# A Mamba scan whose input comes from TensorE in 32-row quarters, four states into four banks

## The chip, the cores and the metric

The kernel runs on one core of a Trainium2 chip. The metric is device time in microseconds (us) of one execution, all phases included. Three runs of the kernel before took 3399.39, 3389.66 and 3397.66 us (median 3397.66).

## The reference, cut to what matters

Two transformer-like layers work on x, 8 sequences of 512 tokens of 256 features. Layer 0 adds to x a Mamba block and an FP4-quantized feed-forward of the normalized x; layer 1 adds a block-sparse attention and a two-deep local attention with its own feed-forward. The change touches the Mamba block (512 inner channels, 16 states, rank 16) and what shares its phase:

```python
u = silu(conv(x_in))                              # [b, l, 512]
x_dbl = u @ W_xproj.T                             # rank 16 | B 16 | C 16
delta = softplus(x_dbl[..., :16] @ W_dt.T + b_dt)
A = -exp(A_log)
def step(h, inp):                                 # one token
    dA = exp(d_t[:, :, None] * A[None])
    h = dA * h + (d_t * u_t)[:, :, None] * B_t[:, None, :]
    y_t = einsum('bdn,bn->bd', h, C_t)
    return h, y_t
y = (ys + D_param * u) * silu(z)
out = y @ W_out.T
```

So for each sequence, channel and state a first-order recurrence runs over 512 tokens. Its input is delta times u (which depends on channel and token) times B (which depends on state and token).

## The kernel before, in words

**Two phases.** Phase one (lines 114 to 796) computes layer 0 for all eight sequences and writes x1 to DRAM. Phase two (from line 799) computes layer 1. They share no work. The diff touches phase one alone.

**The scan.** Channels lie on the 128 partitions, so a sequence has 4 chunks of 128 channels (NC). One step `g` handles two states of one chunk: 8 steps a chunk, STEPS = 32 a sequence, 256 in all. For a step, `decay` (line 655) makes two tiles `da` = exp(delta * A) on ScalarE (ACT); `spread_b` (663) spreads one row of B over all partitions into a PSUM bank, by one bf16 matmul of 512 columns with a selecting matrix `sel`, where B lies in `bp` as three bf16 pieces that add up to its float32 value; `product` (669) multiplies each bank in place by `du` = delta * u on VectorE (DVE); `scan` (677) runs the recurrence on DVE from `da` and the bank into `hh`; `times_c` (680) multiplies both states by C on GpSimd (POOL), where C comes by a broadcast DMA into `cb`; `sum_states` (683) adds the states up by 8 transposes (128x128) on TensorE (PE) into the bank `y`, which turns them to rows.

**The strands.** Everything else of phase one is written as Python generators: `head` (layer norm, input projection, convolution, `xd`, delta and `du` by two chunks at a time), `ffn` (the FP4 feed-forward), `z`, `finish`, `output`, `fp4_weights`, `rotary_tables`. The main loop (765 to 796) calls `step()` once for each scan step; `step` asks every active strand for its next stage, if PSUM banks are free for it (MM = 4 banks in `pmm`; `bu` has 3, `y` one). The wrapper `Ordered` keeps each engine's instructions in the order in which this loop issues them. So every engine's queue is fixed, and an instruction that waits holds up all behind it on its engine. In a loop pass the order around the scan is: `fetch_c(g+2)`, `sum_states` of an older step, `decay(g+1)`, first scan, `spread_b(g+1)` twice, `step()`, `times_c(g-1)`, second scan, `product(g+1)`.

Delta, `du` and u of a sequence are each one tile of 4 chunks, double-buffered. x is loaded once and held until `output` is done with it.

Of the kernel before, what the change touches and what calls it, by code (L numbers as in the profile page):

```python
# [17 lines left out]
P = 128  # L18
NB, L, D = 8, 512, 256
NT = L // P  # L20
# [16 lines left out]
RD, RC, PIECES = 32, 48, (0, 64, 96)  # L37
# [18 lines left out]
def tile_kernel(ctx: ExitStack, tc: tile.TileContext, a: dict, out: bass.AP):  # L56
# [57 lines left out]
    with ExitStack() as s0:  # L114
# [6 lines left out]
        MM = 4  # L121
        pmm = s0.enter_context(tc.tile_pool(name="pmm0", bufs=MM, space=PSUM))
        pbu = s0.enter_context(tc.tile_pool(name="pbu0", bufs=3, space=PSUM))
# [5 lines left out]
        def load_x(b):  # L129
            t = w1.tile([P, NT, D], FP, tag="x", bufs=3, name=f"x_{b}")  # L130
            sp.dma_start(t, a["x"][b].rearrange("(t p) d -> p t d", p=P))
            return t

        x_first = load_x(0)
# [5 lines left out]
        w_dt = w0.tile([RD + DR, DI], FP, name="w_dt")  # L140
        sp.dma_start(w_dt[RD:, :], a["w_dt"])
# [3 lines left out]
        w_o = load(w0, chunks(a["w_o"]), [P, NC, D], "w_o")  # L145


        sel = w0.tile([P, NS, P], BF, name="sel")
        every = w0.tile([P, NS], BF, name="every")

        def constants():
            act.activation(a_neg, a_neg, AF.Exp)
            dve.tensor_scalar(a_neg, a_neg, -1.0, None, ALU.mult)
            dve.tensor_copy(every, ident[:, :NS])
            for at in PIECES[1:]:
                dve.tensor_tensor(every, every, ident[:, at : at + NS], ALU.add)
            for n in range(NS):
                dve.tensor_copy(sel[:, n, :], every[:, n : n + 1].to_broadcast([P, P]))

# [3 lines left out]
        w_d = w0.tile([P, NI, D], FP, name="w_d")  # L163

# [159 lines left out]
        def rotary_tables():  # L328

            for l in range(DEPTH):  # L330
                tab = rot.tile([P, 2, L], FP, tag="e", bufs=2, name="tab")
                tab = tab.rearrange("p i (t d) -> p (i t) d", d=LD).rearrange("p (i t) d -> p i t d", t=NT)
                sp.dma_start(tab, a["rotary"])
                qss = []
                for name in ("q_scale", "k_scale"):
                    qss.append(sm.tile([P, LD], FP, tag="qs", bufs=2, name="qs"))
                    sp.dma_start(qss[-1], a[name][l].unsqueeze(0).to_broadcast([P, LD]))
                yield 0, 0
                yield 0, 0
                dve.tensor_scalar(qss[0], qss[0], 8.0, None, ALU.mult)  # L340
                hd = LD // 2
                lo, hi = slice(0, hd), slice(hd, LD)
                for i, qs in ((0, qss[0]), (2, qss[1])):
                    for at, cols, sc in ((i, lo, lo), (i, hi, hi), (i + 1, lo, hi), (i + 1, hi, lo)):
                        by = qs[:, sc].unsqueeze(1).to_broadcast([P, NT, hd])
                        dve.tensor_tensor(tab[:, at, :, cols], tab[:, at, :, cols], by, ALU.mult)
                        if cols is hi:
                            yield 0, 0
                sp.dma_start(tab_d[l], tab)
                yield 0, 0  # L350

        made, xs, u_, z_, ready, through = {}, {}, {}, {}, set(), set()

        def head(b):

            x = xs[b] = load_x(b) if b else x_first
# [12 lines left out]
            dve.reciprocal(rs, rs)  # L369
            xn = w1.tile([P, NT, D], FP, tag="xn", name="xn")  # L370
# [56 lines left out]
            def silu(c, cv):  # L427
                if c == 0:
                    u_[b] = w1.tile([P, NC, L], FP, tag="u", name="u")
                act.activation(u_[b][:, c, :], cv, AF.Silu)  # L430

            stages = [(project, 0, 1), tap0, taps12, (tap3, 1, 0), silu]
            for i, need in enumerate(skewed(range(NC), stages, 2)):
                while i + 1 == len(stages) and b - 2 in u_:
                    yield 0, 0
                yield need
            u = u_[b]
            yield 1, 1
            ps = pmm.tile([P, L], FP, tag="mm", name="ps_xp")
            for c in range(NC):  # L440
                pe.matmul(ps, w_xp[:, c, :], u[:, c, :], start=(c == 0), stop=(c == NC - 1))
            yield 0, -1
            xd = w1.tile([P, L], FP, tag="xd", bufs=1, name="xd")
            act.copy(xd, ps)
            c_d = dram.tile([NS, L], FP, tag="c_d", name="c_d")
            sp.dma_start(c_d, xd[RC : RC + NS, :])

            bp = w1.tile([P, L], BF, tag="bp", name="bp")
            act.copy(bp, ps)
            yield 0, 0  # L450

            def pieces():
                for at in PIECES[1:]:
                    pool.tensor_tensor(xd[at:, :], xd[at:, :], bp[at:, :], ALU.subtract)
                    yield 0, 0
                    act.copy(bp[at:, :], xd[at:, :])
                    yield 0, 0

            delta = w1.tile([P, NC, L], FP, tag="delta", name="delta")
            du = w1.tile([P, NC, L], FP, tag="du", name="du")
            made[b] = xn, xt, bp, c_d, delta, du

            def rank(c):
                ps = pmm.tile([P, L], FP, tag="mm", name="ps_dt")
                pe.matmul(ps, w_dt[RD:, c * P : (c + 1) * P], xd[RD : RD + DR, :], start=True, stop=True)
                return ps

            def parts(c, ps):  # L470
                act.activation(delta[:, c, :], ps, AF.Relu, bias=b_dt[:, c : c + 1])
                act.activation(ps, ps, AF.Abs, bias=b_dt[:, c : c + 1])
                act.activation(ps, ps, AF.Exp, scale=-1.0)
                act.activation(du[:, c, :], ps, AF.Copy, bias=1.0)
                return ps

            def rests(c, e, ps):
                w = du[:, c, :]
                dve.scalar_tensor_tensor(e[:, c % 2, :], w, 1.0, ps, ALU.subtract, ALU.subtract)

            def second(c0, ps):
                return ps, rank(c0 + 1)

            def third(c0, st):
                e = rot.tile([P, 2, L], FP, tag="e", bufs=2, name="e")
                rests(c0, e, st[0])
                return e, parts(c0 + 1, st[1])

            def fifth(c0, st):
                rests(c0 + 1, *st)  # L490
                return st[0]

            def logs(c0, e):
                w = du[:, c0 : c0 + 2, :]
                act.activation(w, w, AF.Ln)
                return e

            def sums(i):
                def f(c0, e):
                    w = du[:, c0 + i, :]  # L500
                    by.tensor_tensor(w, w, e[:, i, :], ALU.subtract)
                    return e
                return f

            def deltas(i):
                def f(c0, e):
                    c = c0 + i
                    by.tensor_tensor(delta[:, c, :], delta[:, c, :], du[:, c, :], ALU.add)
                    by.tensor_tensor(du[:, c, :], delta[:, c, :], u[:, c, :], ALU.mult)
                    ready.add((b, c))  # L510
                    return e
                return f

            by = pool if b else dve
            rest = pieces()
            stages = [
                (lambda c0, _: rank(c0), 0, 1), parts, (second, 0, 1), (third, 1, 0), lambda _, st: st, (fifth, 1, 0),
                logs, sums(0), sums(1), deltas(0), deltas(1),
            ]
            for need in skewed(range(0, NC, 2), stages, 2 if b else len(stages) - 4):  # L520
                next(rest, None)
                yield need

        def ffn(b):

            x, xn = xs[b], made[b][0]
# [21 lines left out]
            yield from skewed(range(KC), [(turn_x, 0, 1), (put_x, 1, 0)], 1)  # L548
            n = FI // 2
# [30 lines left out]
            def down(t, ht):  # L580
                ps = pmm.tile([P, L], FP, tag="mm", name="ps_d")
                for c in range(NI):
                    m = min(P, FI - c * P)
                    pe.matmul(
                        ps[:, :D], ht[:m, c, :], w_d[:m, c, :], start=(c == 0), stop=(c == NI - 1)
                    )
                return ps

            def add(t, ps):
                dve.tensor_tensor(x[:, t, :], x[:, t, :], ps[:, :D], ALU.add)  # L590

            def begin(t, _):
# [6 lines left out]
                *to_inner(lambda t: q.tile([P, NI, P], FP, tag="ht", name="ht")), (down, 0, 1), (add, 1, 0),  # L599
            ]  # L600
            yield from skewed(range(NT), stages, 5)
# [10 lines left out]
        def output(b):  # L612

            u, x = u_[b], xs[b]

            def tile(i):
                def f(t, ps):
                    if i == 0:
                        ps = pmm.tile([P, L], FP, tag="mm", name="ps_o")
                    for c in range(NC):  # L620
                        pe.matmul(
                            ps[:, i * D : (i + 1) * D], u[:, c, (t + i) * P : (t + i + 1) * P], w_o[:, c, :],
# [7 lines left out]
            def add(t, ps):  # L630
                at = x[:, t : t + 2, :].rearrange("p t d -> p (t d)")
# [4 lines left out]
            yield from skewed(range(0, NT, 2), [(tile(0), 0, 1), tile(1), (add, 1, 0)], 2)  # L636
# [13 lines left out]
        def fetch_c(g):  # L650
            b, c, n = at(g)
            cs[g] = rot.tile([P, 2, L], FP, tag="cb", bufs=3, name="cb")
            sp.dma_start(cs[g], made[b][3][n : n + 2, :].unsqueeze(0).to_broadcast([P, 2, L]))

        def decay(g):
            b, c, n = at(g)
            decays[g] = []
            for i in range(2):
                da = rot.tile([P, L], FP, tag="da", bufs=4, name="da")
                act.activation(da, made[b][4][:, c, :], AF.Exp, scale=a_neg[:, c, n + i : n + i + 1])  # L660
                decays[g].append(da)

        def spread_b(g, i):
            b, c, n = at(g)
            bu = pbu.tile([P, L], FP, tag="bu", name="bu")
# [811 lines left out]
```

## Time and profile before

| | |
|---|---|
| runs, us | 3399.39, 3389.66, 3397.66 |
| profiled execution, span from first to last instruction | 3396.9 us |
| that span beside the median of the runs | 0.8 us below it |
| end of phase one (last add into x, write of x1) | about 1398 us |
| first scan starts, last scan starts | 45.4 us, 1374.5 us |
| mean granted TensorE clock | 0.942 (0.87 up to 1400 us, 0.99 from there) |
| busy to 1400 us: PE, DVE, ACT, POOL | 1042.9, 1256.4, 962.8, 1036.2 us |
| busy from 1400 us: PE, DVE, ACT, POOL | 1931.1, 1166.0, 808.6, 545.3 us |
| 242 ACT table loads in phase one | 1.283 us each |

The page gives the busy time of each engine, the span in 40 slices with a digit for tenths, the chain of work that ended last, and groups of equal instructions. In a group, "busy" is the time that the group's instructions cover, with overlaps counted once; "mean" is one instruction from its start to its end. For pipelined matmuls busy divided by count is far below mean, and it is the better price of one more of them. A float32 matmul appears in the trace as two matmuls, each with its weight load; a transpose as one.

### The profile page before, as it was taken

To read this page: it belongs to the slowest core of one execution; us is meant where nothing else is said; L and a number is where in the kernel's file an instruction comes from. 1 tells how busy PE (TensorE), PEld (TensorE's weight loads), DVE (VectorE), ACT (ScalarE), POOL (GpSimd) and SP (SyncE) were. 2 spreads that over 40 slices of the span, in tenths; PEclk is the share of its full clock that TensorE was granted. 3 is DMA by queue.
4 is the path that set the end of the run, shared out by engine and by line. 5 is a ranking of instruction groups with operands and counts; after the bars stand their busy time and mean duration, and the time that the engine had idled before them with its cause. 6 is when DMAs were issued, how large, how long until landed. Compare 5 with 4: busy or idle time off the path is not lost.

```text
span 3396.9 us, 43346 instructions
## 1 busy us (share of the span) xinstructions
PE 2974.0 (88%) x15235; PEld 1723.3 (51%) x15236; DVE 2422.4 (71%) x4792; ACT 1771.3 (52%) x3500; POOL 1581.5 (47%) x1141
## 2 busy tenths in 40 slices
PE   5667787877777877899999999999999999999998
PEld 2434454545454555555554555555545545545545
DVE  7979898999999999665566466466556557556544
ACT  5666777676767776244254245244334334433533
POOL 3876777787868687333133133123223223312412
PEclk7768898989898889899999999999999999999999
DMA  3322233323232333301111101111110100100100
GB/s 107 120 90 104 97 109 102 125 93 125 96 125 96 119 105 137 108 32 52 40 38 52 45 32 52 46 49 38 42 58 32 64 33 32 64 33 32 58 33 7
DMA packets 88865, 239.55 MB, mean 71 GB/s; under 512 B 9656, under 2 KB 42424, under 8 KB 88648
## 3 DMA queue, kind: packets, MB, share of 16 engines
q1 hardware_dynamic: 87496, 232.59, 19.9%
q10 hardware_dynamic: 1152, 4.19, 0.3%
q8 instruction: 121, 1.98, 0.2%
q14 instruction: 96, 0.79, 0.1%
HBM read 227.05 MB, written 9.70 MB: 70 GB/s over the span
## 4 chain that ended last, share of the span: by engine, by line
PE 59%; DVE 26%; ACT 6%; issue 4%; POOL 4%; DMA 1%; DVEq 0%; SPq 0%; POOLq 0%; ACTq 0%
PE ps_qkv L1131 10%; DVE hh L50 10%; PE ps_g L1310 5%; PE ps_a L1310 4%; PE ps_wo L1274 3%; PE lo L1244 3%; DVE bu L50 3%; PE ps_y L1345 3%; PE ps_w L1328 3%; PE pt L1230 2%; PE y L50 2%; PE ps_ls L1183 2%; PE ps_gu L50 2%; PE ps_d L50 2%; DVE nm L997 2%
## 5 line engine op out<-in xcount | busy, mean ns | idle before, releaser
L50 POOL TENSOR_TENSOR hh<-hh,cb 128x1024 f32<-128x1024 f32 x256 | 604.4, 2363 | 177.5 <-DVE hh L50 109.4
L50 DVE TENSOR_TENSOR_SCAN hh<-da,bu 128x512 f32<-128x512 f32 x512 | 613.7, 1207 | 0.2 <-ACT da L50 0.2
L50 ACT ACTIVATE da<-delta,a_neg 128x512 f32<-128x512 f32 x512 | 355.2, 718 | 290.1 <-DVE hh L50 285.8
L50 PE MATMUL bu<-bp,sel 128*128 128x512 bf16 x511 | 197.3, 423 | 231.3 <-DVE hh L50 230.2
L50 PE MATMUL y<-ident,hh 128*128 128x128 f32 x2048 | 300.9, 298 | 89.9 <-POOL hh L50 89.7
L50 PEld LDWEIGHTS y<-ident,hh 128*128 128x128 f32 x2048 | 264.7, 155 | 179.7 <-POOL hh L50 131.8
L50 DVE TENSOR_TENSOR bu<-du,bu 128x512 f32<-128x512 f32 x512 | 324.9, 681 | 37.1 <-PE bu L50 36.8
L50 ACT ACT_TABLE_LOAD x242 | 310.5, 1283 | 23.9 <-DVE x L50 11.1
L1221 POOL TENSOR_TENSOR pr<-pr,lrs 128x512 f32<-128x512 f32 (+1 forms) x256 | 234.6, 933 | 176.6 <-DVE lrs L1219 137.7
L1150 POOL TENSOR_TENSOR r<-r,r 128x512 f32<-128x512 f32 x128 | 162.8, 1272 | 286.5 <-DVE r L1148 240.8
L1202 ACT ACTIVATE pr<-ps_ls,nm 128x256 f32<-128x256 f32 (+1 forms) x512 | 221.6, 448 | 122.4 <-DVE nm L1196 119.3
L1146 DVE TENSOR_TENSOR r<-ps_qkv,tab 128x512 f32<-128x512 f32 x128 | 88.2, 689 | 199.3 <-ACT sq L1145 195.4
L1316 ACT ACTIVATE gl<-ps_g,b 128x512 f32<-128x512 f32 x96 | 65.9, 687 | 304.1 <-PE ps_g L1310 304.1
L1048 ACT ACTIVATE pt_e<-ps_st 128x512 f32<-128x512 f32 x320 | 166.7, 596 | 107.0 <-PE ps_st L1042 100.8
L886 POOL MEMSET sa<- 128x1 f32 x16 | 1.6, 98 | 450.2 <-DVE sf L1332 356.9
L1091 POOL TENSOR_TENSOR x1s<-x1s,bsum 128x256 f32<-128x256 f32 x32 | 23.2, 724 | 370.3 <-DVE x1s L1090 370.3
L1196 DVE CUSTOM_DVE_ANT_0 ps_ls<-ps_ls,mask 128x256 f32<-128x256 f32 (+1 forms) x512 | 184.3, 422 | 5.7 <-PE ps_ls L1183 4.7
L1310 PE MATMUL ps_g<-hn,wf 128*128 128x512 f32 x384 | 183.0, 599 | 4.0 <-DVE hn L1299 2.6
L1131 PE MATMUL ps_qkv<-wqkv,sf 128*128 128x512 f32 x384 | 182.4, 608 | 0.0
L1131 PE MATMUL ps_qkv<-wqkv,s 128*128 128x512 f32 x384 | 179.8, 604 | 0.2 <-DVE r L1148 0.2
L1317 DVE SCALAR_TENSOR_TENSOR ht<-ps_a,b,gl 128x512 f32<-128x512 f32 x80 | 60.0, 750 | 157.5 <-PE ps_a L1310 157.5
L1230 PE MATMUL pt<-ident,pr 128*128 128x128 f32 x896 | 130.9, 281 | 33.0 <-POOL pr L1221 28.3
(216 smaller groups left out, 6314.5 us busy)
## 6 DMA issues: line engine op xcount, KB each, us to landing
cb<-c_d SPq DMA_DIRECT2D x256, 512.0 KB, 3.6
wqkv<-in_wqkv SPq DMA_DIRECT2D x16, 1536.0 KB, 6.8
wf<-in_wf SPq DMA_DIRECT2D x16, 1408.0 KB, 11.2
wf<-in_wf SPq DMA_DIRECT2D x16, 768.0 KB, 4.7
tab<-tab SPq DMA_DIRECT2D x18, 512.0 KB, 3.6
wo<-in_wo SPq DMA_DIRECT2D x16, 512.0 KB, 3.9
x<-in_x SPq DMA_DIRECT2D x8, 512.0 KB, 5.0
x<-x ACTq DMA_DIRECT2D x8, 512.0 KB
```

The costliest lines, as they stand in the source:

```text
L50: return self.tc.keep_in_program_order(getattr(self.engine, name)(*args, **kwargs))
L1048: act.activation(pt, banks[g], AF.Exp)
L1131: pe.matmul(ps, shifted(s, k, t * P, P), wqkv[:, k, i * IN : (i + 1) * IN], start=(k == 0), stop=(k == KC - 1),)
L1150: pool.tensor_tensor(r1[:, i], r1[:, i], r2, ALU.add)
L1196: last = dve.tensor_tensor_reduce(at, at, msk[:, 2 * P - nk :], -1.0, 3e38, ALU.add, ALU.min, nm[:, i : i + 1])
L1202: act.activation(pr[:, at], banks[r][:, at], AF.Exp, bias=nm[:, i : i + 1], scale=-1.0, accum_out=rs[:, i : i + 1],)
L1221: pool.tensor_tensor(ph, ph, rs.unsqueeze(2).to_broadcast([P, 2, nk]), ALU.mult)
L1230: pe.transpose(pt[:, j * P : (j + 1) * P], pr[:, j * P : (j + 1) * P], ident)
L1244: pe.matmul(o[r * LD : (r + 1) * LD, i * P : (i + 1) * P], lv[:, keys[j], h * LD : (h + 1) * LD], prts[r][:, (i * nkt + j) * P : (i * nkt ...
L1274: pe.matmul(ps, wo[:, c, m * P : (m + 1) * P], ot[:, c, :], start=(c == 0), stop=(c == IN // P - 1),)
L1310: pe.matmul(dst, wf1[:, k, off : off + P], hn[:, k, :], start=(k == 0), stop=(k == KC - 1))
L1328: pe.matmul(ps, wf2[:n, c, m * P : (m + 1) * P], ht[c][:n], start=(c == 0), stop=(c == NHC - 1),)
```

## The change

- `spread_b`, `product`, `sel` and the bf16 pieces are gone. B is turned once for each sequence (`diagonals`): four tiny matmuls bring it to tokens on partitions, and four DVE multiplications with `four` (a 32x32 identity stacked four times) make tiles `bd`, one for each four states: in every 32-row quarter, diagonal matrices of B.
- `du` is turned too, to tokens on partitions (`turned`, `put_du`), in an order of tokens in which each 128-column block holds 32 tokens of each quarter of the sequence.
- `inputs(g)` then makes the scan's input for four states of a chunk at once: 16 float32 matmuls of 32 rows (one quarter), 128 columns, `du`'s block as weights and the diagonals as the moving side. They write one tile of four banks, single-buffered, with the states interleaved: the scan reads it with a step of four elements.
- Two scan steps make a group now: 4 scans, and two calls of `step()` after them, the `inputs` of the next group between these two.
- Banks: 4 for `bu`, 1 for `y`, MM = 3 for the strands (4 before).
- Delta and `du` are held by chunk (HELD = 5), u by chunk (10), `da` 6 deep (4 before). x is loaded twice.
- Active strands are kept sorted by rank: z, finish 0; output 1; the delta chains 2; head 3; ffn 4; weights and tables 5.
- `w_dt` has 128 rows and `ht`, `w_d` are padded with zeros, so that these products use all 128 rows.

```diff
-RD, RC, PIECES = 32, 48, (0, 64, 96)
+RD, RC = 32, 48
+HELD = 5
+QL = P // 4
...
-        MM = 4
+        MM = 3
...
-        pbu = s0.enter_context(tc.tile_pool(name="pbu0", bufs=3, space=PSUM))
+        pbu = s0.enter_context(tc.tile_pool(name="pbu0", bufs=1, space=PSUM))
...
+            dve.tensor_reduce(four, ident.rearrange("p (r n) -> p n r", n=QL), AX.X, ALU.add)
...
-            def pieces():
-                for at in PIECES[1:]:
-                    pool.tensor_tensor(xd[at:, :], xd[at:, :], bp[at:, :], ALU.subtract)
-                    yield 0, 0
-                    act.copy(bp[at:, :], xd[at:, :])
-                    yield 0, 0
...
+            def diagonals():
+                yield 1, 1
+                ps = pmm.tile([P, L], FP, tag="mm", name="ps_bt")
+                for t in range(NT):
+                    pe.matmul(
+                        ps[:, t * NS : (t + 1) * NS], xb[:, t * P : (t + 1) * P], ident[:NS, :NS], start=True, stop=True
+                    )
+                bt = ps[:, : NT * NS].rearrange("p (t n) -> p t n", n=NS)
+                shape = [P, NT, QL, 4]
+                for i in range(NS // 4):
+                    yield (0, -1) if i == NS // 4 - 1 else (0, 0)
+                    bd = rot.tile(shape, FP, tag="bd", bufs=2 * (NS // 4), name="bd")
+                    dve.tensor_tensor(
+                        bd, four.unsqueeze(1).unsqueeze(3).to_broadcast(shape),
+                        bt[:, :, 4 * i : 4 * i + 4].unsqueeze(2).to_broadcast(shape), ALU.mult,
+                    )
+                    diags.append(bd)
...
+            def turned(c, _):
+                ps = pmm.tile([P, L], FP, tag="mm", name="ps_du")
+                for t in range(NT):
+                    pe.transpose(ps[:, t * P : (t + 1) * P], du[b, c][:, t * P : (t + 1) * P], ident)
+                return ps
+
+            def put_du(c, ps):
+                act.copy(du[b, c], ps)
+                ready.add((b, c))
...
-        def spread_b(g, i):
-            b, c, n = at(g)
-            bu = pbu.tile([P, L], FP, tag="bu", name="bu")
-            pe.matmul(bu, sel[:, n + i, :], made[b][2], start=True, stop=True)
-            spreads.setdefault(g, []).append(bu)
-
-        def product(g):
-            b, c, n = at(g)
-
-
-            for bu in spreads[g]:
-                dve.tensor_tensor(bu, made[b][5][:, c, :], bu, ALU.mult)
+        def inputs(g):
+
+            b, c, n = at(g)
+            bu = spreads[g] = spreads[g + 1] = pbu.tile([P, 4, NT, P], FP, tag="bu", name="bu")
+            for t in range(NT):
+                for r in range(4):
+                    rows = slice(r * QL, (r + 1) * QL)
+                    pe.matmul(
+                        bu[:, r, t, :], du[b, c][rows, t * P : (t + 1) * P],
+                        diags_[b][n // 4][rows, t, :, :].rearrange("p n i -> p (n i)"), start=True, stop=True,
+                    )
+
+        def scan(g):
             hs[g] = rot.tile([P, 2, L], FP, tag="h", bufs=4, name="hh")
-
-        def scan(g, i):
-            dve.tensor_tensor_scan(hs[g][:, i, :], decays[g][i], spreads[g][i], 0.0, ALU.mult, ALU.add)
+            bu = spreads[g].rearrange("p r t n -> p (r t n)")
+            for i in range(2):
+                dve.tensor_tensor_scan(
+                    hs[g][:, i, :], decays[g][i], bu[:, 2 * (g % 2) + i :: 4], 0.0, ALU.mult, ALU.add
+                )
...
-            if g + 1 < total:
-                decay(g + 1)
             if now:
-                scan(g, 0)
-            if g + 1 < total:
-                spread_b(g + 1, 0)
-                spread_b(g + 1, 1)
...
-            step()
-            if 0 <= g - 1 < total:
-                times_c(g - 1)
-            if now:
-                scan(g, 1)
-            if g + 1 < total:
-                product(g + 1)
+                scan(g)
+            if g + 2 < total:
+                decay(g + 2)
+            if g % 2 == 0:
+                if now:
+                    times_c(g)
+            else:
...
+                step()
+                if now:
+                    times_c(g)
+                if g + 1 < total:
+                    inputs(g + 1)
+                if now and (g - 1) % (NS // 2):
+                    sum_states(g - 1)
+                step()
```

## Prediction, made before the changed kernel was run

> **What bounds the kernel now.** I began with the 40 slices, since the diff touches only phase one (up to about 1398 us, the first 16.5 slices).
>
> ```profile
> PE   5667787877777877899999999999999999999998
> ...
> DVE  7979898999999999665566466466556557556544
> ACT  5666777676767776244254245244334334433533
> POOL 3876777787868687333133133123223223312412
> PEclk7768898989898889899999999999999999999999
> ```
>
> In phase one VectorE (DVE) is at 9 and the others at 6 to 8; from slice 17 TensorE (PE) takes over. A phase one that ends earlier moves phase two forward as it stands. The next view is busy time in one inner stretch as long as one sequence: scans start from 45.4 to 1374.5 us, over eight sequences, so a sequence takes **167 us**.
>
> ```profile
> 880.00:1047.00 167.00, 128.25 (x575) 84.41 (x574) 155.66 (x203) 122.40 (x168) 129.51 (x76) 0.89 0.32 109
> ```
>
> The columns after the length are PE, PE weight loads, DVE, ACT, POOL, granted clock, DMA share, GB/s. DVE is busy 155.7 of 167 us (93%), no other over 78%. Then the groups of instructions:
>
> ```profile
> L50 POOL TENSOR_TENSOR hh<-hh,cb 128x1024 f32<-128x1024 f32 x256 | 604.4, 2363 | 177.5 <-DVE hh L50 109.4
> L50 DVE TENSOR_TENSOR_SCAN hh<-da,bu 128x512 f32<-128x512 f32 x512 | 613.7, 1207 | 0.2 <-ACT da L50 0.2
> ...
> L50 PE MATMUL bu<-bp,sel 128*128 128x512 bf16 x511 | 197.3, 423 | 231.3 <-DVE hh L50 230.2
> L50 PE MATMUL y<-ident,hh 128*128 128x128 f32 x2048 | 300.9, 298 | 89.9 <-POOL hh L50 89.7
> ...
> L50 DVE TENSOR_TENSOR bu<-du,bu 128x512 f32<-128x512 f32 x512 | 324.9, 681 | 37.1 <-PE bu L50 36.8
> ```
>
> Scans never wait for their inputs (0.2 us idle before 512 of them), while PE waits 230 us and ACT 286 us for DVE. So phase one runs at DVE's pace. The multiplication into `bu`, 324.9 us, is what the change takes off DVE.
>
> **The change, engine by engine, for one sequence** (16 groups of four states):
>
> *DVE*: 64 products go, 324.9/8 = 40.6 us; four `bd` multiplications come, at the product's 0.68 us, 2.7 us. 155.7 - 40.6 + 2.7 = **117.8**. The scan now reads PSUM with a step of four elements over four banks. No row shows such a read. A scan takes 2.36 ns an element, an ordinary product from PSUM 1.33 ns: a slower read hides until it reaches 2.36. I take nothing; the bound above is the product's time added once, 0.68 us a scan (43 us a sequence). I see no reason for a gain.
>
> *POOL*: two subtractions for pieces of B go, 18.5/8 = 2.3 us: **127.2**. The `du` product now reads and writes runs of 32 elements; I take it as it was (1.27 us, four times), at worst twice that, 5 us.
>
> *ACT*: casts to bf16 go (14.5/8 = 1.8); `put_du` comes (4 x 0.58 = 2.3) and the copy `xb` (0.6); four logarithms of 512 (0.6 each) replace two of 1024 (1.06): +0.3; the built order has 232 table loads for 242: -1.6. **122.2**.
>
> *PE*: the broadcasts go, 197.3/8 = 24.7 us. Per group come 16 float32 matmuls, in the trace 32 halves with 32 weight loads. The nearest rows are in phase two:
>
> ```profile
> L1230 PE MATMUL pt<-ident,pr 128*128 128x128 f32 x896 | 130.9, 281 | 33.0 <-POOL pr L1221 28.3 <-ACT pr L1202 2.4
> L1244 PE MATMUL lo<-prt,lv 128*64 128x128 f32 x1792 | 128.4, 279 | 0.0
> L1044 PE MATMUL ps_st<-qt,kt 32*128 32x256 f32 x768 | 55.1, 400 | 0.0
> ```
>
> The third has the same 32-row quarters at 256 columns: 55.1/768 = 72 ns a half, so 36 ns at 128 if columns alone count: 32 x 36 = 1.15 us a group, the lower end. The first is 128 columns on the whole array, 146 ns: 32 x 146 = 4.7 us, the upper end, with quarters not running side by side. The second has 128 columns and two tiles side by side: 72 ns, 2.3 us. The new form has the columns of the second and the packing of the third, so I take the middle of these two, 1.7 us, and 0.4 for entering and leaving quarters (next paragraph): 2.1 us a group, 33.6 a sequence. Transposes of `du` add 16 x 0.147 = 2.4 and `ps_bt` 0.6. Products that now use all rows save about 2.1 (64-row halves of `ps_d` 348 ns for 236, 16-row halves of `ps_dt` 661 for 505 of `ps_xp`, eight each). 128.3 - 24.7 + 33.6 + 2.4 + 0.6 - 2.1 = **138.1**; the bounds are 116 (1.15 a group, no switch) and 180.
>
> The switch has a row: in the chain of waits, eight halves of `ps_qkv` take 3.63 us between two blocks of quarters, 3.44 where whole-array transposes stand ahead of them: 0.19 us, counted twice a group.
>
> ```profile
> 1454.86 3.63 PE ps_qkv L1131 x8
> 1461.59 3.44 PE ps_qkv L1131 x8
> ```
>
> The Trainium skill, TensorEngine Tiling (Array Packing), Key Properties, speaks against the change here: switching the tiling mode drains TensorE. The trace agrees that there is a price, 0.19 us, and it makes 6 us of a sequence's PE time; by the rule alone, with a full drain of one 281 ns transpose each way, it would be 9 us and the total about 3 us a sequence more.
>
> *DMA and queues*: x is loaded twice (0.5 MB at about 5 us, eight times). The second load waits, on SP's queue, for the write of the previous x (about 4 us); behind it stand the `cb` loads, issued two steps (about 10 us) ahead and landing in 3.6. That covers it; without cover, 4 us a sequence on POOL.
>
> **The wait that is added.** The four banks of `bu` are single. The next group's 16 matmuls can start only after the fourth scan, and the next scan only after them: some 2.3 us with hand-over, in which DVE has only the strand work queued there. By the built order, a middle sequence has between its groups of scans 0.7, 3.6, 0.9, 2.9, 6.8, 2.9, 2.3, 1.5, 1.4, 6.2, 2.8, 2.6, 4.1, 1.8, 1.0 and 0.7 us of it: the shortfalls below 2.3 add up to about 8 us, if PE is free at that moment. On PE, waiting matmuls hold back the state sums of this group and all strand products behind them; for the sums waits `finish`, for the products ACT.
>
> **The sum.** No engine is at 93% in the next place: loads are 118, 127, 122 and 138. How closely do queues follow each other? I took each engine's instructions from the built order, group by group, priced by the rows above, and added up the busiest engine's load. Where all engines must meet after every group, a sequence takes 164 us; after every second, 158; after every fourth, 143. The same count on the kernel before gives 174, 167 and 165, and it takes 167: meeting after every second group fits, and it is also how far `hh` (four buffers, two groups) reaches. In the changed kernel the busiest engine alternates (PE 7, POOL 4, DVE 3, ACT 2 of 16 groups), so this costs far more than before. I take a fifth of the way to the loose count: **155 us**. Gain: 8 x 12 = 96 us. At the end the last feed-forward trails by one gate and up product more (6 us PE): +6. 3396.9 - 96 + 6 = **3307 us** for the profiled execution, whose span lies 0.8 us below the median of the runs; I add nothing for that.
>
> **The rivals.**
> 1. *Engines bind, not their meeting*: sequences at the loose count, 143 us. 3397 - 192 + 6 = 3211. For it: strands are ordered by urgency, `da` is 6 deep. Against it: three banks for strands instead of four, and `bu` single.
> 2. *Coupling eats it*: PE, now the busiest, stands behind POOL for `y` sums (already 90 us idle there before, and 132 on weight loads) and behind DVE for `bu`; each blocked sum delays the matmuls for the next scan. At 164 to 167 us a sequence: 3397 - 24 + 6 to 3403, about 3385.
> 3. *Slower: the quarters don't run side by side*, because each half must load its weights first and has only 128 columns to hide that behind. Place: the 16 matmuls of a group, in the gap between scans. At 4.7 us PE has about 180 us a sequence: 3397 + 8 x 13 + 6 = 3507 at least, about 3590 with PE at 95%. It decides from where PE reaches some 155 us, at 3.2 us a group. For it: no row has 32 rows at 128 columns. Against it: in `ps_st` the overlap is about 3.5-fold (72 ns against 257 for `ps_ao`, 256 columns on the whole array).
> That the change does not do what it says I rule out by the built order: 512 products are gone and 2048 matmuls stand there.
>
> **Chances.** Forecast (150 to 161 us a sequence, 3267 to 3355): 0.42. Rival 1 (3180 to 3267): 0.23. Rival 2 (3355 to 3411): 0.20. Rival 3, with a slower strided scan (43 us on DVE would give about 161, worth less than the rest, but with coupling also above 167): 0.15, 3411 to 3590. The range 3205 to 3420 leaves out about 0.07 below and 0.13 above. About 0.3% (10 us) is what a measurement of this kernel can tell from no change: of rival 2, 0.11 lies below 3387, 0.06 within, 0.03 above. Faster 0.42 + 0.23 + 0.11 = 0.76, same 0.06, slower 0.15 + 0.03 = 0.18.
>
> **What would show it.** Right: a sequence at about 155 us with no engine above 90% busy; DVE's idle before scans named "PE bu", some 10 to 25 us a sequence; 16 matmuls in 1.7 to 2.1 us; scans still at 1.21 us. Wrong: scans at 1.4 us or more; PE above 150 us a sequence; a `bu` group near 1.1 us with PE below 125 and DVE or POOL above 90% (rival 1); POOL waited for by PE's sums longer than before, and `bu` late for that (rival 2).

## The result

The changed kernel takes **3413.33 us** (median of five runs, 3409.29 to 3418.56), the kernel before beside it 3397.66 (3389.66 to 3399.39): a ratio of **1.0053, 95% interval 1.0037 to 1.0069**. It is slower by half a per cent, where 3307 us and a gain were forecast. The profiled execution has a span of 3413.4 us, before 3396.9.

The slices of the changed kernel's page:

```profile
PE   5667778777777878899999999999999999999998
...
DVE  6768686868686868665565466466566557556544
ACT  6575767676777677244254245244334334433533
POOL 3786686867777778332133133123123213312412
```

VectorE has come down from mostly 8 and 9 to 6 and 8 in phase one, as forecast, and no other engine has gone up by more than a tenth in any slice of it. Phase one still ends in the same slice. The stretch of one sequence says it in numbers (length, then PE, weight loads, DVE, ACT, POOL, clock, DMA share, GB/s):

```profile
880.00:1047.00 167.00, 129.32 (x1040) 94.07 (x1039) 124.91 (x140) 117.98 (x166) 124.38 (x73) 0.92 0.34 111
```

Every engine is under 78% busy. A middle sequence (the fourth to the sixth) takes 167 us, where before it took 164; the mean over all eight is 166 in both kernels, since the scans run from 46.5 to 1376.4 us, before from 45.4 to 1375.7. **31 us less work of VectorE in this stretch (155.7 to 124.9) has bought nothing.** The groups that the change touches:

```profile
L52 POOL TENSOR_TENSOR hh<-hh,cb 128x1024 f32<-128x1024 f32 x256 | 606.5, 2382 | 344.4 <-DVE hh L52 182.4
L52 DVE TENSOR_TENSOR_SCAN hh<-da,bu 128x512 f32<-128x512 f32 x512 | 581.4, 1197 | 109.1 <-PE bu L52 98.4
...
L52 PE MATMUL bu<-bd,du 32*128 32x128 f32 x4096 | 176.2, 317 | 55.5 <-DVE hh L52 55.5
```

The scan takes 1197 ns (before 1207): its read with a step of four costs nothing here. The sixteen float32 matmuls of a group take 176.2/128 = 1.38 us (the forecast took 2.1). So the prices of the new instructions were right or too high. What costs is idle time.

**Where the time stands.** From the starts of the scans in the timeline, fourteen of the sixteen groups of a middle sequence of the changed kernel follow one another after 9.2 us on average (before 10.2). The last two take **23.3 and 14.7 us**: some 19 us too many. In the kernel before no group of the fourth to the seventh sequence takes over 12.7. This is VectorE in the long one (start, duration, instruction, in brackets the idle time ahead and what ended it):

```profile
878.83 4.55 DVE L52 TENSOR_TENSOR_SCAN hh<-da,bu 128x512 f32<-128x512 f32 x4 [2.18 <-PE bu L52]
883.30 0.66 DVE L52 TENSOR_TENSOR bd<-four,ps_bt 128x512 f32<-128x512 f32 x1
883.88 0.68 DVE L52 SCALAR_TENSOR_TENSOR e<-du,ps_dt 128x512 f32<-128x512 f32 x1
884.47 4.41 DVE L52 TENSOR_SCALAR q_m<-q_m 128x704 bf16<-128x704 bf16 x1
889.00 0.89 DVE L52 SCALAR_TENSOR_TENSOR q_v<-q_v,q_m 128x704 f32<-128x704 f32 x1
...
895.24 0.52 DVE L52 TENSOR_TENSOR h<-h,ps_gu 128x352 f32<-128x352 f32 x1 [3.40 <-PE ps_gu L52]
901.54 0.69 DVE L52 SCALAR_TENSOR_TENSOR e<-du,ps_dt 128x512 f32<-128x512 f32 x1 [5.78 <-ACT du L52]
902.15 1.21 DVE L52 TENSOR_TENSOR_SCAN hh<-da,bu 128x512 f32<-128x512 f32 x1
```

Between the scan that ends at 883.4 and the one at 902.2 there are only strands, and VectorE works 9.5 of these 18.8 us. In them the next sequence's first chunk is made ready (`ps_dt`, `e`, logarithm, `du`, transposes, copy). They stand there because of the main loop (lines 790 and 791): while the chunk needed two steps ahead is not ready, `step()` is called without a scan. Followed through the program, the list of strands gives the changed kernel three such steps at each of the seven passages to a next sequence, 21 in all; the kernel before has 7 in all, five and two at its first two passages and none later. And a strand is refused for want of a PSUM bank 268 times in the changed kernel and 12 times in the kernel before: `bu` holds four banks, `y` one, and MM has gone from 4 to 3.

One more thing is in this fence. `q_m`, a bf16 operation, takes 4.41 us. GpSimd beside it:

```profile
884.02 4.67 POOL L52 TENSOR_TENSOR hh<-hh,cb 128x1024 f32<-128x1024 f32 x2
```

It ends 0.2 us after GpSimd's two products. The shortest `q_m` of the kernel before, of either width, took 0.28 us.

This `q_m` also stands at the head of what the next scan waits for. Behind it come `q_v` and `h`; `h` releases TensorE at 890.37, whose queue then runs without a pause through `ps_gu`, `bu`, `y`, `ps_gu`, `ps_z` and `ps_dt`; and that `ps_dt` belongs to the next sequence's second chunk:

```profile
896.69 1.02 PE L52 MATMUL ps_dt<-xd,w_dt 128*128 128x512 f32 x2
...
897.75 0.69 ACT L52 ACTIVATE delta<-ps_dt,b_dt 128x512 f32<-128x512 f32 x1 [0.26 <-PE ps_dt L52]
...
900.91 0.60 ACT L52 ACTIVATE du<-ps_dt 128x512 f32<-128x512 f32 x1
```

The `e` at 901.54, which VectorE waits 5.78 us for, is the second chunk's. The scan's own input was in its banks by 893; the scan stands behind that `e` in VectorE's queue.

### The profile page after: what moved, and what is told of

It is laid out like the page before. It is cut to its first block, busy times and chain, and to the rows that moved or that the text cites. A ratio compares the mean times of both kernels' runs of the same rounds, so it can differ in the third digit from the quotient of the medians.

```text
span 3413.4 us, 50356 instructions
## 1 busy us (share of the span) xinstructions
PE 3002.3 (88%) x19012; PEld 1818.1 (53%) x19012; DVE 2213.4 (65%) x4294; ACT 1766.6 (52%) x3522; POOL 1569.8 (46%) x1128
## 4 chain that ended last, share of the span: by engine, by line
PE 49%; DVE 8%; ACT 2%; POOL 1%; issue 1%; DMA 1%; DVEq 0%; ACTq 0%; POOLq 0%; SPq 0%
PE ps_qkv L1153 10%; PE ps_g L1332 5%; PE ps_a L1332 4%; PE ps_wo L1296 3%; PE lo L1266 3%; PE ps_y L1367 3%; PE ps_w L1350 3%; PE pt L1252 2%; PE ps_ls L1205 2%; PE pt_qk L1144 2%; DVE nm L1019 1%; PE ps_st L1066 1%; PE o L1048 1%; PE ps_qk L961 1%; DVE ps_ls L1218 1%
## 5 line engine op out<-in xcount | busy, mean ns | idle before, releaser
L52 DVE TENSOR_TENSOR_SCAN hh<-da,bu 128x512 f32<-128x512 f32 x512 | 581.4, 1197 | 109.1 <-PE bu L52 98.4
L52 ACT ACTIVATE da<-delta,a_neg 128x512 f32<-128x512 f32 x512 | 347.1, 717 | 196.7 <-DVE hh L52 194.8
L52 PE MATMUL y<-ident,hh 128*128 128x128 f32 x2048 | 293.2, 292 | 50.5 <-POOL hh L52 50.4
L52 PEld LDWEIGHTS y<-ident,hh 128*128 128x128 f32 x2048 | 249.9, 151 | 96.6 <-POOL hh L52 62.8
L52 PE MATMUL bu<-bd,du 32*128 32x128 f32 x4096 | 176.2, 317 | 55.5 <-DVE hh L52 55.5
L52 PEld LDWEIGHTS bu<-bd,du 32*128 32x128 f32 x4096 | 150.7, 217 | 122.1 <-issue 91.4
```

Source lines behind the costliest of these rows:

```text
L52: return self.tc.keep_in_program_order(getattr(self.engine, name)(*args, **kwargs))
```

## The experiments

**Theory 1**: the missing bank makes the next sequence's chain late, and the steps without a scan that follow are the lost 19 us. **Theory 2**: the sums (the sixteen products of `inputs`) into the single `bu`, issued behind strand products on TensorE, come late, and this couples the engines. **Theory 3**: products by C, now in bursts of two beside VectorE's strand work, hold its quantizing operations. **Rival** to all: the engines' coupling costs the same in whatever order. Each ratio below is to the kernel before run beside it (medians of 3392 to 3399 us); differences in us are between medians.

### The order of the strands, and the place of the sums

`urgent` (3347.82 us, ratio to before 0.9869, 0.985 to 0.9888) changes two ranks:

```diff
-            begin(diagonals(), 2)
+            begin(diagonals(), 0)
...
-                begin(skewed([c], stages, 1), 2)
+                begin(skewed([c], stages, 1), 0)
```

> The changed kernel with the strands of the next sequence's diagonals and of its delta chunks put at the front of the list (rank 0 in place of 2), so that they get a PSUM bank before the others. In the changed kernel the first chunk of each next sequence is ready three strand steps late, and three steps without a scan stand before its first group (seven sequence starts, 21 steps); with this edit only the first two starts have them (6 steps). Theory 1, the missing fourth bank makes that gap: the last two groups of a sequence took 23.3 and 14.7 us where the other fourteen took 9.2 on average, some 19 us too many, so five sequences give back up to 95 us: 3413 goes to 3320 to 3350, and a sequence to 150 to 155 us. Rival, the work of the strands is the same and only moves into the fourteen other groups, which are bound by waits between engines: within 15 us of 3413. Theory 2 (the sums wait for bu, that stands behind the strands' products on TensorE) expects no more than the bubble's own waits for bu back, under 20 us.

It takes 65 us off. The third to the seventh sequence, which now end without such steps, take 148 to 154 us; the second, which still has them, 199. That is what theory 1 expected, at the edge of its range (some 14 us a sequence where the two groups had 19 too many); the rival falls.

`inputs_first` (3443.87 us, 1.0137, 1.011 to 1.0164):

```diff
+                if g + 1 < total:
+                    inputs(g + 1)
                 step()
                 if now:
                     times_c(g)
-                if g + 1 < total:
-                    inputs(g + 1)
```

> The changed kernel with the sixteen products of a group issued ahead of the first strand step of the odd pair, so that on TensorE they no longer stand behind strand products which themselves wait for ScalarE and VectorE. Theory 2: VectorE's idle time before the scans for bu (98.4 us over the kernel) falls to under 40 and the time by 40 to 60 us, to 3355 to 3375. Theory 1 (the three steps without a scan per sequence): bu comes earlier, but the three steps stay, as the order of the strands is the same: the time falls by under 20 us. Theory 3 (VectorE's quantizing operations are held by GpSimd's products on the port that the two share): no change in their means, 1314 and 1768 ns.

It is 30 us slower, which no theory expected. Waits of the stretch from 379 to 1214 us (engine, tile, who ended it: us in total, times, longest) in the changed kernel and in this run; first the changed kernel, VectorE:

```profile
DVE hh L52 <- PE bu L52: 76.1, 50, 4.8
DVE e L52 <- ACT du L52: 42.3, 10, 5.8
DVE h L52 <- PE ps_gu L52: 36.6, 15, 3.4
...
DVE x L52 <- PE ps_o L52: 8.7, 5, 1.7
```

then `inputs_first`, VectorE and TensorE:

```profile
DVE x L52 <- PE ps_d L52: 44.9, 16, 4.7
DVE h L52 <- PE ps_gu L52: 43.2, 26, 3.6
...
DVE x L52 <- PE ps_o L52: 35.6, 10, 4.9
...
DVE hh L52 <- PE bu L52: 3.1, 6, 1.5
```

```profile
PE bu L52 <- DVE hh L52: 100.4, 53, 4.3
```

The wait for `bu` is gone (76.1 to 3.1 us), as theory 2 wanted. But the sums now stand ahead of the strands' products and wait for the four banks (100.4 us, 8.6 in the changed kernel), and VectorE waits for those products instead. Theory 2 falls as a reason of the loss: by this order the wait is moved from one queue to another, not removed. Theory 3 expected the quantizing operations unchanged; `q_m` fell from 1314 to 814 ns and `q_v` rose from 1768 to 1986.

`urgent_inputs`, both edits (3421.79 us, 1.0084, 1.0069 to 1.0099):

> Both edits together. Theory 1 and theory 2 as two separate costs: the gains add, 3413 less some 70 and some 40, about 3300. If the wait for bu is only the other face of the same gap, no more than the better of the two alone. Rival, coupling whatever the order: all of them within 15 us of 3413.

Nothing adds. The second edit takes back 74 us, more than the 65 that the first gave.

`urgent2` (**3287.17 us, 0.9682**, 0.966 to 0.9703) is `urgent` and

```diff
-                for _ in range(3):
+                for _ in range(1):
                     yield 0, 0
...
-                for k, f in ((-3, z), (1, finish)):
+                for k, f in ((-5, z), (1, finish)):
                     if k in gates:
-                        begin(f(*gates[k]), 0)
+                        begin(f(*gates[k]), 3 if f is z else 0)
```

> As the first, with the four delta chunks of the next sequence begun two steps apart in place of four, and the gate products (z) begun one pair of groups earlier at the rank of the projections, so that only one sequence start has steps without a scan (4 steps in all). Theory 1: the gap goes from two more starts than in the first run, a further 20 to 30 us: 3300 to 3320. Rival: no further change, within 10 us of the first run, or a loss where the earlier strands take banks from the others.

It beats both kernels, by more than theory 1 expected. One sequence:

```profile
880.00:1027.00 147.00, 124.88 (x1041) 90.45 (x1041) 121.85 (x140) 113.87 (x166) 125.43 (x73) 0.95 0.37 123
```

147 us in place of 167, with nearly the same work on every engine and the same three banks. No run tells the three parts of the edit (spacing, start and rank of `z`) apart. The second to the seventh sequence all take 146.7 to 146.8 us; sixteen groups, 9.2 us each, what the fourteen undisturbed ones of the changed kernel took.

### The bank by itself, and the gap by itself

`four_banks` (3302.45 us, 0.972, 0.9705 to 0.9735) leaves the ranks alone and gives the bank back:

```diff
-        MM = 3
+        MM = 4
...
-            bu = spreads[g] = spreads[g + 1] = pbu.tile([P, 4, NT, P], FP, tag="bu", name="bu")
+            bu = spreads[g] = spreads[g + 1] = pbu.tile([P, 3, NT, P], FP, tag="bu", name="bu")
...
-                for r in range(4):
+                for r in range(3):
...
-                    hs[g][:, i, :], decays[g][i], bu[:, 2 * (g % 2) + i :: 4], 0.0, ALU.mult, ALU.add
+                    hs[g][:, i, :], decays[g][i], bu[:, (2 * (g % 2) + i) % 3 :: 3], 0.0, ALU.mult, ALU.add
```

> The changed kernel with its fourth bank for the strands given back, and their order of rank as it was: the sums take three banks, the products of the fourth row quarter are left out, and the scan reads every third element of three banks instead of every fourth of four (as many elements, by the same matmuls otherwise, 12 instead of 16 in a group). By the list of strands only the first sequence start then has steps without a scan (2). Theory 1, the missing bank makes the gap: sequences of 147 to 152 us from the second on, 3270 to 3320. Rival, the rank of the delta chunks matters by itself (it shortens some other wait), and banks don't: sequences near 167, the time over 3380. TensorE loses a quarter of the products (some 0.3 us in a group if they took a quarter of it, 5 us in a sequence), which under the rival is all that this run could gain.

The time is in theory 1's range; the third to the seventh sequence take 148 to 155 us, a little over its 147 to 152, and the second 172. The left-out products are no rival: the 128 groups of twelve matmuls keep TensorE busy for 170.2 us, those of sixteen for 176.2.

```profile
L52 PE MATMUL bu<-bd,du 32*128 32x128 f32 x3072 | 170.2, 309 | 75.8 <-DVE hh L52 75.6
```

Strands are refused a bank 19 times here. In `urgent2` it is still 198 times, and it is faster: what counts is which strand is refused. So the bank is the reason, and order can pay for it.

`urgent2_gap` (3334.93 us, 0.9822, 0.9806 to 0.9838):

```diff
+            if g % STEPS == STEPS - 2 and STEPS < g < total - STEPS:
+                for _ in range(3):
+                    step()
             while g + 2 < total and not able(g + 2):
                 step()
```

> The kernel of the run urgent2 (3287 us) with the three steps without a scan put back by hand, at the same place (before the last pair but one of a sequence) in six of the seven sequences that are followed by another. The ranks and the banks are those of urgent2. Theory 1, it is the steps without a scan that cost: 10 to 19 us each time, 3350 to 3400. Rival, the order of the strands is what gained, not the missing gap: within 20 us of 3287, since the same work of the strands is only done earlier.

48 us for six gaps, 8 each: less than theory 1 expected and more than its rival. Three steps without a scan do cost, but on average 8 of some 20 us (the sequences with a gap are longer by 5 and by 10 to 12 us in turn). What makes up the other 12 in the changed kernel was not separated by a run. Its long group has one candidate that the trace shows: `q_m` at the head of the chain took 4.41 us, where the two of its width with no GpSimd instruction beside them took 0.34; all five `q_m` of over 4 us stand in such long groups. With half of GpSimd's product (`half_times_c`, below) this group takes 20.1 us in place of 23.3.

### The sums' waits and GpSimd's products

`sums_once` (3353.52 us, 0.9866, 0.985 to 0.9882):

```diff
             b, c, n = at(g)
+            if n:
+                spreads[g] = spreads[g + 1] = spreads[g - 1]
+                return
...
-            del hs[g], decays[g], spreads[g]
+            del hs[g], decays[g]
```

> The changed kernel with the sums made for the first group of a chunk only; the other three groups scan the same bu again (three quarters of the products are left out, 48 of 64 in a chunk). The order of everything else and the gap at the end of a sequence stay. Theory 1: the gap of some 19 us stays and with it most of the time; VectorE's 98 us of idle time before scans fall to a quarter, and no more than 60 us come back: 3350 to 3390. Theory 2 (the wait for bu on its single set of banks is what couples the engines): sequences of 150 us or less, under 3310.

Sequences of 157 us, whose last two groups still take 22.5 and 14.5; VectorE's wait for `bu` falls from 98.4 to 30.0 us over the kernel. Three quarters of the sums, their waits included, are worth 10 us a sequence; the gap stands. This is theory 1's side.

`half_times_c` on the changed kernel (3321.27 us, 0.9777, 0.9762 to 0.9791), `before_half_c` on the kernel before (3340.51, 0.9838, 0.9825 to 0.9852) and `urgent2_half_c` on `urgent2` (3222.3, 0.9488, 0.9476 to 0.9501) have one edit:

```diff
-            pool.tensor_tensor(hs[g], hs[g], cs.pop(g), ALU.mult)
+            pool.tensor_tensor(hs[g][:, 0, :], hs[g][:, 0, :], cs.pop(g)[:, 0, :], ALU.mult)
```

> The changed kernel with GpSimd's product by C made for one of the two states of a pair only (the other state is left as the scan gave it), so that each of the 256 products takes about 1.2 in place of 2.38 us. Theory 3: the means of VectorE's two quantizing operations fall from 1314 and 1768 ns to at or below those of the kernel before (882 and 1119), some 8 us in a sequence, and the time by 40 to 70 us. Theory 1: the gap is a chain of steps on ScalarE, VectorE and TensorE; shorter operations in it shorten it by the few us that they wait in it, so a sequence stays over 155 us and the time over 3340.

> The kernel before the change with GpSimd's product by C made for one of the two states only (the other is left as the scan gave it), the control of the run half_times_c, in which the same edit took 92 us off the changed kernel. Theory 3 as the reason of the changed kernel's loss (its products by C stand in bursts beside VectorE's quantizing operations, those of the kernel before do not): before gains far less, under 30 us. Theory 1 alone (the gap of the missing bank is the reason; what GpSimd holds of VectorE is paid in both kernels): before gains as much, 60 to 110 us, since VectorE bounds it at 155.66 us of 167 and its quantizing operations fall from 882 and 1119 ns to some 600 and 1110.

> The kernel of urgent2 with the same cut. If the gap and what GpSimd holds of VectorE are two separate costs, they add: 3287 less 60 to 90, 3200 to 3230, and a sequence of 136 to 140 us. If the cut only shortened the gap, within 20 us of 3287.

The edit gains 92, 58 and 65 us. The quantizing operations of 704 columns (busy, mean ns of one), first before, then the changed kernel, then `half_times_c`:

```profile
L50 DVE SCALAR_TENSOR_TENSOR q_v<-q_v,q_m 128x704 f32<-128x704 f32 x34 | 47.4, 1395 | 3.2
L50 DVE TENSOR_SCALAR q_m<-q_m 128x704 bf16<-128x704 bf16 x34 | 32.9, 967 | 10.7 <-ACT q_m L50 10.7
```

```profile
L52 DVE SCALAR_TENSOR_TENSOR q_v<-q_v,q_m 128x704 f32<-128x704 f32 x34 | 56.1, 1649 | 3.6 <-DVE q_m L52 0.5
L52 DVE TENSOR_SCALAR q_m<-q_m 128x704 bf16<-128x704 bf16 x34 | 44.6, 1312 | 25.4 <-ACT q_m L52 25.4
```

```profile
L52 DVE SCALAR_TENSOR_TENSOR q_v<-q_v,q_m 128x704 f32<-128x704 f32 x34 | 35.9, 1055 | 3.6 <-DVE q_m L52 0.5
L52 DVE TENSOR_SCALAR q_m<-q_m 128x704 bf16<-128x704 bf16 x34 | 17.2, 505 | 23.2 <-ACT q_m L52 23.2
```

All of VectorE's operations of these two kinds took 116.1 us before and 178.8 in the changed kernel; with the edit 78.4 and 93.9. So the holding is real and grew by 63 us of VectorE's time, of which the edit takes back 47. As a reason of the loss, the control sizes it: before gains 58 us by the same edit, the changed kernel only 34 more, and `urgent2`, without the gap, about as much as before (65). By this, theory 3 is worth some 34 of the 106 us between forecast and result, perhaps somewhat more, as the edit removes half of the product; and some of it lies inside the gap (3.2 us of each long group), so that it does not add to theory 1's price. What of each gain is the hold and what GpSimd's own shorter work isn't told apart. Of the three expectations: the changed kernel kept sequences of 157 us, as theory 1 said, but gained more than either theory (92 us, where theory 3 had 40 to 70); before gained 58, near theory 1's 60 to 110 and not under 30; and `urgent2` with the edit reached 3222, inside its range, with sequences of 137 to 146 us where 136 to 140 were expected.

`urgent_each` (3401.12 us, 1.0012, 1.0003 to 1.0022) begins the delta chunks three steps apart (the changed kernel four, `urgent2` two), takes the ranks of `urgent2` except that of `diagonals`, and puts one strand step after each pair of scans:

```diff
-                begin(skewed([c], stages, 1), 2)
-                for _ in range(3):
+                begin(skewed([c], stages, 1), 0)
+                for _ in range(2):
...
             if g % 2 == 0:
+                step()
                 if now:
                     times_c(g)
             else:
...
-                for k, f in ((-3, z), (1, finish)):
+                for k, f in ((-5, z), (1, finish)):
                     if k in gates:
-                        begin(f(*gates[k]), 0)
+                        begin(f(*gates[k]), 3 if f is z else 0)
...
                     sum_states(g - 1)
-                step()
```

> The changed kernel with ranks and spacing that leave steps without a scan at one sequence start only (4), and one strand step after each pair of scans, where the changed kernel has two after every second pair. GpSimd's products by C then no longer come in bursts of two. Theory 3: VectorE's quantizing operations fall towards 882 and 1119 ns and the time below urgent2's 3287, to 3220 to 3270. Rival (the sums' four banks are free again only after the fourth scan, so a strand step between the pairs only delays them): within 15 us of 3287 or above it.

Only the first passage to a next sequence still has steps without a scan, and yet the run is 114 us behind `urgent2`: the rival was right, and of the two quantizing operations only `q_m` fell to its value of before (867 ns; `q_v` took 1877). VectorE's longest waits (379 to 1214 us):

```profile
DVE hh L52 <- PE bu L52: 196.8, 67, 10.7
DVE u L52 <- PE ps_y L52: 13.9, 5, 3.7
```

The wait for `bu` is 58.7 us in the same stretch of `urgent2`. The step that was moved had stood between the sums and the next scan and covered them. `urgent_each_in` (3311.67 us, 0.9748, 0.9725 to 0.9771) puts the sums ahead of the remaining step, by the same edit as in `inputs_first`:

> The run urgent_each (3401 us) with the sums issued ahead of the strand step that follows the fourth scan, so that this step stands between the sums and the next scan. There VectorE sat idle for bu for 197 us of 835, since nothing of its own was left between the fourth scan, which frees the four banks, and the next scan. If that lost cover is its whole loss, the wait falls under 40 us of 835, and with products by C that no longer come in bursts of two the time goes below urgent2's 3287, to 3220 to 3280. If the sums at the front of TensorE's queue only hold the strands' products back, as in the run inputs_first (where TensorE waited 100.4 us for the scans ahead of bu), 3300 to 3400.

90 us come back, but the wait only falls to 93.6 us, and TensorE waits 74.4 for the banks (37.4 in `urgent_each`). The time lies in the second range (3300 to 3400), near its lower end: the cover was most of the loss, and the single set of banks remains. The burst was not worth breaking up: `q_v` of 704 columns takes 2192 ns here (`urgent2` 2094 in this stretch).

## Why the prediction was wrong, step by step

- **DVE, 117.8 us a sequence**: 124.9 in the same stretch. The scan was right (no cost). The missing 7 us are the quantizing operations beside GpSimd's products, whose duration was taken from the kernel before: in the fourth to the sixth sequence they took 14.1 us each before and 21.4 in the changed kernel.
- **POOL 127.2, ACT 122.2**: 124.4 and 118.0. Near enough.
- **PE, 138.1**: 129.3. The term that was mis-sized is the group of sixteen matmuls, 2.1 us forecast and 1.38 measured, near the lower end (1.15): 16 x 0.7 = 11 us. The quarters do run side by side, so rival 3 falls. Two slips beside it: the lower bound of 116 doesn't follow from its own terms (with 1.15 us a group they give 123), and the 0.4 us for the switch rests on one pair of rows, which the timeline puts 0.10 us apart (3.70 and 3.60) where the chain has 0.19; no run priced the switch by itself.
- **The wait that is added**, 10 to 25 us a sequence before scans for `bu`: 76.1 us in five sequences, 15 each. Right, and `inputs_first`, `urgent_each` and `urgent_each_in` show that its cover is the strand step behind the sums.
- **The second load of x**: no DMA is among the waits of VectorE or GpSimd there. Right.
- **The sum is the step that failed**: "meeting after every second group fits", 155 us. The count added up each group's instructions as loads of engines. In fourteen groups it was even too high (9.2 us on average, 147 a sequence, which `urgent2` reaches). In the last two it saw strand work that can lie beside other work, where the program has a chain that the loop waits for: three steps without a scan, with VectorE idle half of 18.8 us, and two groups of 23.3 and 14.7 us. What the count would have needed was in the built order, the extra steps at a sequence's end; "three banks for strands instead of four" stood in the working as an argument against rival 1, with no price. Its price is 111 us by `four_banks` against the changed kernel (3302 against 3413), more than the whole forecast gain of 96.
- **What the count was fitted to** was off too. The 167 us are a mean that includes the first three sequences (191, 178 and 171 us; over all eight it is 166); a middle one took 164. That is nearer to the count's 165, for meeting after every fourth group, and for the changed kernel this looser count gave 143, nearer to the 147 of `urgent2` than 155 is.
- **The tail, +6 us**: from the last scan's end to phase two's first matmul 40.0 us, before 30.0: +10. Phase two itself then took 1996.9 us, before 1991.2, with unchanged code (1991 to 2001 in the other runs); nothing here explains those 5.7. With the scans' end 0.7 later, these are the 16.5 us between the two spans.
- **Rival 2** has the right number of a sequence (164 to 167) and the wrong mechanism: it let TensorE's blocked sums delay the scans in every group. They don't; the groups got shorter. That it came close in time, and that 3413 still lies within the stated 3205 to 3420, is luck.

No run speaks for another main reason of the loss than theory 1, but its sizes were off in several: `urgent2` gained more than it expected, `urgent2_gap` lost less, `half_times_c` gained more, and `inputs_first` lost where it expected a small gain. Open are how the other 12 us of a gap divide between what the trace shows in it, and how the gains of the half products divide.

## What to carry to other kernels

When a change takes a buffer or a bank from a shared pool, price it: follow the scheduler's list in both versions, count how often work is refused, and look whether a chain that the main loop waits for gets later. An average load per engine can't show this; one group that takes 23 us among fourteen of 9 can. And the work that is issued between a request (here the sums) and the instruction that needs its result covers the request's time: moving either one moves the wait.

## What the runs showed of the hardware

VectorE's two quantizing operations (`q_v`, both inputs in SBUF, and `q_m`, in bf16) are held while GpSimd works on SBUF tiles: `q_m` took 0.28 us at its shortest in the changed kernel and 4.42 at its longest, through two products of GpSimd end to end. In the changed kernel the 15 `q_v` of 704 columns with no GpSimd instruction beside them took 0.89 us each, the other 19 took 2.25 on average. Operations that read one input from PSUM are not held: the mean of the scan lies between 1.19 and 1.21 us and that of `e` between 0.67 and 0.69 in every run, bursts or not. The Trainium skill, SBUF — State Buffer, Who interferes with whom, states the rule (the port pair of VectorE and GpSimd is an exclusive lock held for the whole instruction); these runs agree, and add that the hold went through two instructions that followed at once.

Thirty-two float32 halves of 32 rows and 128 columns, each with its own weights, take 1.38 us, where halves on the whole array take 146 ns each in phase two of the kernel before (4.7 us for as many). The Trainium skill, TensorEngine Tiling (Array Packing), Key Properties, says that tiles load weights and multiply independently of one another; the trace agrees, with a factor of 3.4.
